# A forward transform that handles two slabs per step instead of one

## The chip, the cores and the metric

The kernel runs on one core of a Trainium2 chip. The metric is the device time of one launch in microseconds (us), taken as the median of several runs. A core has a matrix engine (TensorE, "PE" in the profile; its weight loads are the row "PEld"), a vector engine (VectorE, "DVE"), a scalar engine (ScalarE, "ACT"), a general engine (GpSimd, "POOL") and a synchronisation engine (SyncE, "SP"). Each has its own instruction queue and works it off in order. SP, ACT and POOL also issue DMA transfers. Matrix products read on-chip memory and write their sums into PSUM banks, which another engine then copies out.

## The reference, cut to what matters

The model has two layers over x of shape 4 x 512 x 128 x 64 (batch, time T, features, channels). The change touches only the second:

```python
trend = _moving_average(x, KERNEL)          # 25 wide, along time
seasonal = x - trend
xf = jnp.fft.rfft(seasonal, axis=1)
xs = xf[:, :M]                              # M = 128 modes
W = w_real + 1j * w_imag
ys = jnp.einsum('bmnc,cmk->bknc', xs, W)
...
filt = jnp.fft.irfft(yf, n=T, axis=1)
return trend + filt
```

The forward transform of the seasonal part is linear in x, so it can be a product of fixed matrices with x: for each batch, 128 modes, real and imaginary, from 512 times.

## The kernel before, in words

The first layer (`layer0`) runs until about 2795 us of the profile and is not touched. It ends by writing its result to `x4`, one DRAM tensor of 512 x 8192 per batch. The second layer (`layer1`, L845 on) treats two batches at a time (a group). For each group it runs three stages in a row: `transform` of both batches, `mix` (the channel-wise products with W), and `invert` of both batches. So there are two forward stages in the program, one from 2796 us to 2941 us and one from about 3292 us to 3437 us.

A batch is cut into 16 slabs of 512 columns. `transform` handles one slab per turn of its loop, 32 slabs per group:

- `slab` (L893) loads 512 x 512 values (1 MB) into an `xin` tile through SP. The tag "big" has five buffers, which `mix` also uses for its tiles `w` and `invert` for its own slabs.
- L906 and L907 (POOL queue) load the first and last 12 times of the slab, 24 rows, into an `edge` tile, and L908 (ACT) copies these rows to partitions 32 to 55, so that the same rows stand on two row groups of the array. `edge` has two buffers.
- L912 (DVE) forms the sum and the difference of the slab's two halves in time, `uv[0]` and `uv[1]`; L917 (DVE) forms sum and difference of the two halves of `uv[0]`, called `ev`. All of these have two buffers per tag.
- L921 (PE): four products of `uv[1]` with 64-column weights, the odd modes. L928 (PE): four products of `ev` with 32-column weights, the even modes. L935 (PE): four products of `edge` with 64-column weights on the row groups at 0 and 32, which correct the ends of the moving average. All twelve add into two PSUM banks `pf`, one real, one imaginary.
- L937 (ACT) copies the two banks into `xf`, the spectrum of the group, in which `mix` then reads every slab.

PSUM has four banks with the tag "a" and four with the tag "b". The forward transform uses only "a", that is, two slabs' worth. The order of PE's instructions is the order in which they are written (`manual_schedule`); for the other engines a scheduler places the instructions, and it may move one slab's work past another's where the buffers allow.

`mix` loads its weights `w` (1 MB each, L945, SP) into buffers of the tag "big", and POOL negates two parts of each at L948 before PE uses them. As built, POOL's queue has the first four of these negations between the edge loads of the last slabs: the order is edges of slab 27, `w` 0, edges of slab 28, `w` 1, edges of slab 29, `w` 2, edges of slab 30, `w` 3, edges of slab 31. PE's first products of `mix` are L955 and L959.

Of the kernel before, what the change touches and what calls it, by code (L numbers as in the profile page):

```python
# [10 lines left out]
F32 = mybir.dt.float32  # L11
AF = mybir.ActivationFunctionType
ALU = mybir.AluOpType
# [3 lines left out]
P = 128  # L17
T = 512
NF = 128
H = 64  # L20
D = NF * H
NCH = D // P
SL = 512
NS = D // SL
# [4 lines left out]
M = 128  # L29
KMA = 25  # L30
HALO = KMA // 2
# [813 lines left out]
def layer1(ctx, tc, x4, wri, dftv, dftd, dfte, idfte, idfto, avg, avgh, out):  # L845
# [7 lines left out]
    nc = tc.nc  # L853
# [5 lines left out]
    io = ctx.enter_context(tc.tile_pool(name="io", bufs=2))  # L859
# [4 lines left out]
    def load(pool, eng, name, src):  # L864
        t = pool.tile(list(src.shape), F32, name=name)
        eng.dma_start(t, src)
        return t

    dftv_sb = load(dft, nc.sync, "dftv_sb", dftv)
    dftd_sb = load(dft, nc.sync, "dftd_sb", dftd)  # L870
    dfte_sb = load(dft, nc.sync, "dfte_sb", dfte)
# [5 lines left out]
    def bank(tag):  # L877
        return ps.tile([P, SL], F32, tag=tag, name=tag)


    def by_c(row):
        return row.rearrange("p (a c l) -> p a l c", c=H, l=2)

    def by_n(row):
        return row.rearrange("p (a l c) -> p a l c", c=H, l=2)
# [7 lines left out]
    def slab(b, s):  # L893
        xin = io.tile([P, NT, SL], F32, tag="big", name="xin", bufs=5)
        nc.sync.dma_start(
            xin, x4[b][:, s * SL : (s + 1) * SL].rearrange("(c p) d -> p c d", p=P)
        )
        return xin

    def transform(b, xf):  # L900

        for s in range(NS):
            c = slice(s * SL, (s + 1) * SL)
            xin = slab(b, s)
            edge = io.tile([P, SL], F32, tag="edge", name="edge")
            nc.gpsimd.dma_start(edge[0:HALO, :], x4[b][0:HALO, c])  # L906
            nc.gpsimd.dma_start(edge[HALO : 2 * HALO, :], x4[b][T - HALO : T, c])  # L907
            nc.scalar.copy(edge[32 : 32 + 2 * HALO, :], edge[0 : 2 * HALO, :])  # L908
            uv = []
            for op in (ALU.add, ALU.subtract):  # L910
                t = io.tile([P, 2, SL], F32, tag=f"uv{len(uv)}", name="uv")
                nc.vector.tensor_tensor(t, xin[:, 0:2, :], xin[:, 2:4, :], op)  # L912
                uv.append(t)
            pf = [bank("a"), bank("a")]
            ev = io.tile([P, 2, SL], F32, tag="ev", name="ev")
            for k, op in enumerate((ALU.add, ALU.subtract)):
                nc.vector.tensor_tensor(ev[:, k, :], uv[0][:, 0, :], uv[0][:, 1, :], op)  # L917
            for i in range(2):
                for r in range(2):
                    h = 1 - r  # L920
                    nc.tensor.matmul(  # L921
                        pf[r][h * H : (h + 1) * H, :], lhsT=dftd_sb[:, i, r, :], rhs=uv[1][:, i, :],
                        start=(i == 0), stop=False,
                    )
            for k in range(2):
                for r in range(2):
                    q = r * H + k * H // 2
                    nc.tensor.matmul(  # L928
                        pf[r][q : q + H // 2, :], lhsT=dftv_sb[:, k, r, :], rhs=ev[:, k, :], start=True, stop=False
                    )  # L930
            for r in range(2):
                at = slice(32 * r, 32 * r + 2 * HALO)
                for h in range(2):
                    hs = slice(h * H, (h + 1) * H)
                    nc.tensor.matmul(pf[r][hs, :], lhsT=dfte_sb[at, hs], rhs=edge[at, :], start=False, stop=True)  # L935
            for r in range(2):
                nc.scalar.copy(by_c(xf[:, r, c]), by_n(pf[r]))  # L937

    def mix(xf):

# [83 lines left out]
    with tc.manual_schedule(engines={nc.tensor.engine}):  # L1024
        for b0 in range(0, B, G):
            xf = spec.tile([P, G, 2, D], F32, tag="xf", name="xf")
            for b in range(G):
                transform(b0 + b, xf[:, b, :, :])
            mix(xf)
            for b in range(G):  # L1030
                invert(b0 + b, xf[:, b, :, :])


def _constants():

    a = np.zeros((T, T))
    for t in range(T):
        for s in range(t - HALO, t + KMA - HALO):
            a[t, min(max(s, 0), T - 1)] += 1.0 / KMA
    around = np.zeros((T, T))  # L1040
    for t in range(T):
        for s in range(t - HALO, t + KMA - HALO):
            around[t, s % T] += 1.0 / KMA
    k, n = MODES, np.arange(T)
    angle = 2.0 * np.pi * ((k[:, None] * n[None, :]) % T) / T
    waves = np.stack([np.cos(angle), -np.sin(angle)])

    dft = waves @ (np.eye(T) - around)
    at = np.concatenate([np.arange(HALO), np.arange(T - HALO, T)])
    edge = (waves @ (around - a))[:, :, at]  # L1050
    dfte = np.zeros((2, 32, M))
    dfte[0, : 2 * HALO] = edge[0].T
    dfte[1, : 2 * HALO] = np.roll(edge[1], H, axis=0).T
    weight = np.where(k == 0, 1.0, 2.0)[:, None] / T
    idft = waves * weight
    idft[1, k == 0] = 0.0
    q = H // 2
    idfte = np.concatenate([idft[r, i : i + q, :P] for i in (0, q) for r in range(2)])
    idfto = np.concatenate([idft[r, H:, : T // 2] for r in range(2)])
    tiles = [slice(i * P, (i + 1) * P) for i in range(NT)]  # L1060
    avg = np.stack([a[s, s].T for s in tiles], axis=1)
    avgh = np.zeros((NT, 32, P))
    for j, s in enumerate(tiles):
        at = [t for t in range(s.start - HALO, s.start) if t >= 0]
        at += [t for t in range(s.stop, s.stop + HALO) if t < T]
        avgh[j, : len(at)] = a[s][:, at].T
    c = {
        "dftv": dft[:, :H, :P].reshape(2, 2, H // 2, P).transpose(3, 1, 0, 2),
        "dftd": dft[:, H:, : T // 2].reshape(2, H, 2, P).transpose(3, 2, 0, 1),
        "dfte": dfte.reshape(2 * 32, M),  # L1070
        "idfte": idfte,
        "idfto": idfto.reshape(M, 2, P),
        "avg": avg,
        "avgh": avgh.reshape(P, P),
    }
    return {n: v.astype(np.float32) for n, v in c.items()}


def _inputs(x, i):
# [22 lines left out]
    for rows, parts in ((MODES, ("w_real", "w_imag")), (IMAG, ("w_imag", "w_real"))):  # L1102
# [16 lines left out]
        "fb2": np.concatenate([i["ffn_b2"]] * 2)[:, None],  # L1119
        "wri": wri.reshape(H, M, 2, 2, M).transpose(1, 0, 2, 3, 4),  # L1120
        **_constants(),
    }
    return {n: np.ascontiguousarray(v) for n, v in a.items()}
# [17 lines left out]
```

## Time and profile before

| | |
|---|---|
| median of 3 runs | 3773.87 us (3772.81 to 3791.47) |
| span of the profiled execution | 3800.7 us |
| first forward stage, first product to first product of `mix` | 2804.05 to 2941.03 us |
| second forward stage, the same | 3297.58 to 3437.38 us |
| busy in 2880 to 2900 us | PE 20.00, DVE 18.87, ACT 8.91, POOL 5.01 us of 20 |
| moved by DMA in 2880 to 2900 us | 284 GB/s |
| median landing of an edge load | 4.6 us (L906), 4.4 us (L907) |

The profile is of one execution; its span is 0.7% longer than the median of the timed runs, and no separate time is given for that execution. All times in the text are counted from the start of that span. PE is busy 96% of the span, but busy time of a pipelined engine does not say that it is at its limit, so the stages have to be read one by one.

### The profile page before, as it was taken

What the parts mean: (1) busy time and instruction counts of PE and PEld (TensorE: products, weight loads), DVE (VectorE), ACT (ScalarE), POOL (GpSimd) and SP (SyncE); (2) the same over time, 40 slices, a digit from 0 to 9 for tenths busy, and PEclk for the clock granted to TensorE, in tenths of its full rate; (3) what the DMA queues carried; (4) which work ended last, traced back from release to release, by engine and by line L of the source; (5) the groups of instructions that cost most, each with busy time, mean ns of one, the idle gap of its engine ahead of it and who ended that gap; (6) DMA issues with size and microseconds to landing.
All of it is one profiled execution on the core that took longest, in us unless ns stands there. A gap on an engine that the chain in (4) does not pass through costs nothing. (4 is left out here: it accounts for less than half of the span.)

```text
span 3800.7 us, 44873 instructions
## 1 busy us (share of the span) xinstructions
PE 3636.3 (96%) x15945; PEld 1345.5 (35%) x15945; DVE 2683.6 (71%) x3498; ACT 1761.2 (46%) x2491; POOL 513.3 (14%) x782
## 2 busy tenths in 40 slices
PE   9989999999999999999999988999989999999998
PEld 4433322223333223333322322333322843327533
DVE  4445559976777896677789799755567277892677
ACT  0013336645656565566656678867744210142100
POOL 0000012210011221011122221100012000131001
PEclk9999989999999899999999999999999999999999
DMA  9867647786874788787478677545567478993687
GB/s 310 272 203 242 229 146 264 254 288 241 287 280 169 247 285 287 251 278 278 172 258 282 205 249 262 202 155 177 183 222 246 146 236 295 309 294 140 205 296 264
DMA packets 429175, 912.80 MB, mean 240 GB/s; under 512 B 33240, under 2 KB 83608, under 8 KB 424856
## 3 DMA queue, kind: packets, MB, share of 16 engines
q1 hardware_dynamic: 351024, 636.87, 49.7%
q0 software_dynamic: 75776, 271.62, 20.5%
q8 instruction: 127, 2.08, 0.2%
q10 hardware_dynamic: 2152, 1.45, 0.1%
q14 instruction: 96, 0.79, 0.1%
HBM read 641.31 MB, written 268.50 MB: 239 GB/s over the span
## 5 line engine op out<-in xcount | busy, mean ns | idle before, releaser
L729 PE MATMUL pa<-mid,w_sb 128*64 128x512 f32 x2048 | 500.2, 609 | 37.2 <-DVE x4t L734 37.2
L734 DVE SCALAR_TENSOR_TENSOR x4t<-pa,fb_sb,x 128x512 f32<-128x512 f32 x252 | 188.4, 748 | 345.7 <-PE pa L729 345.6
L722 ACT ACTIVATE mid<-m,fb_sb 128x1024 f32<-128x1024 f32 x256 | 285.1, 1114 | 280.5 <-PE m L718 280.2
L718 PE MATMUL m<-x,w_sb 64*128 64x512 f32 x1008 | 290.4, 649 | 0.4 <-ACT mid L722 0.4
L722 ACT ACTIVATE mid<-c,fb_sb 128x1024 f32<-128x1024 f32 x256 | 283.2, 1106 | 1.5 <-PE c L718 1.5
L718 PE MATMUL c<-x,w_sb 64*128 64x512 f32 x1008 | 263.4, 596 | 1.3 <-ACT mid L722 1.3
L729 PEld LDWEIGHTS pa<-mid,w_sb 128*64 128x64 f32 x2048 | 125.0, 136 | 379.9 <-issue 250.8
L406 PE MATMUL a<-xp,wx 128*128 128x512 f32 x512 | 240.7, 596 | 0.5 <-DVE me L268 0.5
L986 ACT COPY two<-a 128x512 f32<-128x512 f32 x64 | 37.5, 586 | 425.0 <-PE a L981 425.0
L1009 PE MATMUL b<-xin,avg_sb 128*128 128x512 f32 x512 | 230.8, 593 | 2.3 <-DVE xin L1015 2.3
L1015 DVE TENSOR_TENSOR xin<-b,pm 128x512 f32<-128x512 f32 x256 | 159.1, 684 | 95.6 <-PE b L1012 80.7
L567 ACT ACTIVATE sq<-x 128x1024 f32<-128x1024 f32 x128 | 135.0, 1054 | 180.5 <-DVE x L564 180.5
L620 DVE SCALAR_TENSOR_TENSOR to<-kd,vec,to 128x510 f32<-128x510 f32 (+1 forms) x272 | 197.8, 746 | 16.0 <-ACT to L616 10.4
L695 ACT ACTIVATE kd<-kd,vec 128x512 f32<-128x512 f32 x256 | 193.3, 809 | 3.1 <-DVE kd L687 3.1
L891 DVE COPY xf<-b 128x256 f32<-128x256 f32 x128 | 54.4, 425 | 185.3 <-PE b L955 173.2
L912 DVE TENSOR_TENSOR uv<-xin 128x1024 f32<-128x1024 f32 x128 | 155.4, 1227 | 39.4 <-DMA xin<-x 18.9
L251 PE MATMUL st<-x,ones 128*32 128x512 f32 x512 | 169.4, 611 | 13.3 <-DVE x L564 13.1
L743 PEld LDWEIGHTS pt<-ident,x4t 128*128 128x128 f32 x1024 | 107.7, 141 | 208.7 <-ACT mid L722 152.5
L528 DVE TENSOR_TENSOR x<-a,xp 128x1024 f32<-128x1024 f32 x128 | 156.2, 1220 | 33.6 <-PE a L526 31.1
L620 DVE SCALAR_TENSOR_TENSOR z<-x,vec,z 128x511 f32<-128x511 f32 x240 | 175.8, 745 | 5.7 <-ACT z L616 2.3
L526 PE MATMUL a<-rst,wo_sb 64*128 64x512 f32 x512 | 153.1, 672 | 27.2 <-DVE x L528 23.2
L743 PE MATMUL pt<-ident,x4t 128*128 128x128 f32 x1024 | 168.8, 288 | 1.5 <-ACT ob L750 1.5
(241 smaller groups left out, 6532.8 us busy)
## 6 DMA issues: line engine op xcount, KB each, us to landing
xp<-in_xt SPq DMA_DIRECT2D x256, 512.0 KB
xin<-x SPq DMA_DIRECT2D x128, 1024.0 KB
kh<-to SPq DMA_DIRECT2D x156, 512.0 KB
x<-x POOLq DMA_DIRECT2D x128, 512.0 KB, 4.4
kx<-x SPq DMA_DIRECT2D x128, 512.0 KB
x<-ob POOLq DMA_DIRECT2D x64, 1024.0 KB, 6.3
out<-xin POOLq DMA_DIRECT2D x64, 1024.0 KB, 7.1
x<-x SPq DMA_DIRECT2D x96, 512.0 KB
```

Of the source, the lines that this page charges most:

```text
L251: nc.tensor.matmul(st[32 * q : 32 * q + 32, :], lhsT=ones, rhs=src[:, j, :], start=first, stop=last,)
L406: nc.tensor.matmul(pa[:, k, :], lhsT=wq[:, j, k * P : (k + 1) * P], rhs=xp[:, j, :], start=first and j == 0, stop=last and j == 1,)
L528: nc.vector.tensor_tensor(x1, at, xp, ALU.add)
L620: tap = nc.vector.scalar_tensor_tensor(to[:, j, k:], xr[:, j, : SL - k], vec[:, w, c], to[:, j, k:], ALU.mult, ALU.add)
L695: tc.keep_in_program_order(nc.scalar.activation(d[:, j, :], d[:, j, :], AF.Identity, bias=vec[:, B4, c], scale=vec[:, G4, c]))
L718: nc.tensor.matmul(pm[:, h, :], lhsT=w1_sb[hs, m * P : (m + 1) * P], rhs=x3[hs, :], start=True, stop=True)
L722: nc.scalar.activation(mid, pm, AF.Gelu_apprx_tanh, bias=fb1_sb[:, m : m + 1])
L729: nc.tensor.matmul(pa[h * H : (h + 1) * H, :], lhsT=w2_sb[:, m, :], rhs=mid[:, h, :], start=(m == 0), stop=(m == 1),)
L734: nc.vector.scalar_tensor_tensor(x4t, pa, fb2_sb, x3s[c // 2][:, c % 2, :], ALU.add, ALU.add)
L743: nc.tensor.transpose(pt[:, t, :], x4t[:, t * P : (t + 1) * P], ident)
L1009: nc.tensor.matmul(po[j], lhsT=avg_sb[:, j, :], rhs=xin[:, j, :], start=True, stop=False)
L1015: nc.vector.tensor_tensor(by_n(xin[:, j, :]), by_n(po[j]), by_c(pm[j % 2][:, j // 2, :]), ALU.add)
```

## The change

The loop now takes two slabs per turn (a pair). One `edge` tile holds the edge rows of both slabs, at partitions 0 and 32 for the first and at 64 and 96 for the second, and the weights `dfte` are stored twice so that they stand on all four row groups. The edge loads and their ACT copies are as many as before. On VectorE the same four operations per slab are made, with the difference (now `v`) written ahead of the sum (now `u`) in the program. On TensorE the products of a pair come by kind: eight of L921's kind, eight of L928's, then eight edge products, which use four row groups and two column halves. Pairs use the PSUM tags "a" and "b" in turn, four banks each. The copies out of PSUM come after the pair.

```diff
--- before.py
+++ after.py
@@ -899,42 +899,55 @@
 
     def transform(b, xf):
 
-        for s in range(NS):
-            c = slice(s * SL, (s + 1) * SL)
-            xin = slab(b, s)
+        for g in range(NS // 2):
             edge = io.tile([P, SL], F32, tag="edge", name="edge")
-            nc.gpsimd.dma_start(edge[0:HALO, :], x4[b][0:HALO, c])
-            nc.gpsimd.dma_start(edge[HALO : 2 * HALO, :], x4[b][T - HALO : T, c])
-            nc.scalar.copy(edge[32 : 32 + 2 * HALO, :], edge[0 : 2 * HALO, :])
-            uv = []
-            for op in (ALU.add, ALU.subtract):
-                t = io.tile([P, 2, SL], F32, tag=f"uv{len(uv)}", name="uv")
-                nc.vector.tensor_tensor(t, xin[:, 0:2, :], xin[:, 2:4, :], op)
-                uv.append(t)
-            pf = [bank("a"), bank("a")]
-            ev = io.tile([P, 2, SL], F32, tag="ev", name="ev")
-            for k, op in enumerate((ALU.add, ALU.subtract)):
-                nc.vector.tensor_tensor(ev[:, k, :], uv[0][:, 0, :], uv[0][:, 1, :], op)
-            for i in range(2):
-                for r in range(2):
-                    h = 1 - r
-                    nc.tensor.matmul(
-                        pf[r][h * H : (h + 1) * H, :], lhsT=dftd_sb[:, i, r, :], rhs=uv[1][:, i, :],
-                        start=(i == 0), stop=False,
-                    )
+            uv, ev, pf = [], [], []
+            for k in range(2):
+                s = 2 * g + k
+                c = slice(s * SL, (s + 1) * SL)
+                xin = slab(b, s)
+                q = k * H
+                nc.gpsimd.dma_start(edge[q : q + HALO, :], x4[b][0:HALO, c])
+                nc.gpsimd.dma_start(edge[q + HALO : q + 2 * HALO, :], x4[b][T - HALO : T, c])
+                nc.scalar.copy(edge[q + 32 : q + 32 + 2 * HALO, :], edge[q : q + 2 * HALO, :])
+                u = io.tile([P, 2, SL], F32, tag="uv0", name="u")
+                v = io.tile([P, 2, SL], F32, tag="uv1", name="v")
+                nc.vector.tensor_tensor(v, xin[:, 0:2, :], xin[:, 2:4, :], ALU.subtract)
+                nc.vector.tensor_tensor(u, xin[:, 0:2, :], xin[:, 2:4, :], ALU.add)
+                t = io.tile([P, 2, SL], F32, tag="ev", name="ev")
+                for i, op in enumerate((ALU.add, ALU.subtract)):
+                    nc.vector.tensor_tensor(t[:, i, :], u[:, 0, :], u[:, 1, :], op)
+                uv.append(v)
+                ev.append(t)
+                pf.append([bank("ab"[g % 2]), bank("ab"[g % 2])])
+            for k in range(2):
+                for i in range(2):
+                    for r in range(2):
+                        h = 1 - r
+                        nc.tensor.matmul(
+                            pf[k][r][h * H : (h + 1) * H, :], lhsT=dftd_sb[:, i, r, :], rhs=uv[k][:, i, :],
+                            start=(i == 0), stop=False,
+                        )
+            for k in range(2):
+                for i in range(2):
+                    for r in range(2):
+                        q = r * H + i * H // 2
+                        nc.tensor.matmul(
+                            pf[k][r][q : q + H // 2, :], lhsT=dftv_sb[:, i, r, :], rhs=ev[k][:, i, :],
+                            start=True, stop=False,
+                        )
             for k in range(2):
                 for r in range(2):
-                    q = r * H + k * H // 2
-                    nc.tensor.matmul(
-                        pf[r][q : q + H // 2, :], lhsT=dftv_sb[:, k, r, :], rhs=ev[:, k, :], start=True, stop=False
-                    )
-            for r in range(2):
-                at = slice(32 * r, 32 * r + 2 * HALO)
-                for h in range(2):
-                    hs = slice(h * H, (h + 1) * H)
-                    nc.tensor.matmul(pf[r][hs, :], lhsT=dfte_sb[at, hs], rhs=edge[at, :], start=False, stop=True)
-            for r in range(2):
-                nc.scalar.copy(by_c(xf[:, r, c]), by_n(pf[r]))
+                    at = slice(k * H + 32 * r, k * H + 32 * r + 2 * HALO)
+                    for h in range(2):
+                        hs = slice(h * H, (h + 1) * H)
+                        nc.tensor.matmul(
+                            pf[k][r][hs, :], lhsT=dfte_sb[at, hs], rhs=edge[at, :], start=False, stop=True
+                        )
+            for k in range(2):
+                s = 2 * g + k
+                for r in range(2):
+                    nc.scalar.copy(by_c(xf[:, r, s * SL : (s + 1) * SL]), by_n(pf[k][r]))
 
     def mix(xf):
 
@@ -1067,7 +1080,7 @@
     c = {
         "dftv": dft[:, :H, :P].reshape(2, 2, H // 2, P).transpose(3, 1, 0, 2),
         "dftd": dft[:, H:, : T // 2].reshape(2, H, 2, P).transpose(3, 2, 0, 1),
-        "dfte": dfte.reshape(2 * 32, M),
+        "dfte": np.concatenate([dfte.reshape(2 * 32, M)] * 2),
         "idfte": idfte,
         "idfto": idfto.reshape(M, 2, P),
         "avg": avg,
```

## The prediction

> **What bounds the kernel now.** I read the page first: PE is busy 96% of the span, which settles nothing. The chain that ended last, cut to the first forward stage, shows what that stage waits for:
>
> ```profile
> 2876.36 1.87 PE a L921 x8
> 2878.23 1.00 PE a L928 x8
> 2879.22 1.02 PE a L935 x8
> 2880.24 1.87 PE a L921 x8
> ...
> 2913.20 1.24 DVE uv L912
> 2914.44 0.02 issue
> 2914.45 4.12 DMA w<-in_wri
> 2918.57 0.50 POOL edge L906
> 2919.07 4.50 DMA edge<-x
> 2923.57 0.14 issue
> 2923.70 2.44 PE a L935 x8
> 2926.15 3.61 PE a L921 x8
> ```
>
> The columns are start, length in us, and what was late. PE alone carries the chain: 1.87 + 1.00 + 1.02 = 3.88 us a slab. Near the end a detour appears: an edge load stands behind a negation of `w` in POOL's queue, that behind the load of `w`, so PE gets its edge rows late, and then runs at half speed. From the first product of slab 1 (2811.21) to that of slab 28 (2918.98) a slab takes 107.8 / 27 = 3.99 us.
>
> Second, how near the next engines are. The windows view (busy us of PE, PEld, DVE, ACT, POOL; granted clock, DMA share, GB/s) and VectorE's timeline while PE does not yet hold it back:
>
> ```profile
> 2880.00:2900.00 20.00, 20.00 (x126) 4.44 (x124) 18.87 (x22) 8.91 (x15) 5.01 (x10) 1.00 0.91 284
> ```
>
> ```profile
> 2828.46 2.36 DVE L912 TENSOR_TENSOR uv<-xin 128x1024 f32<-128x1024 f32 x2
> 2830.74 1.29 DVE L917 TENSOR_TENSOR ev<-uv 128x512 f32<-128x512 f32 x2
> 2832.06 2.36 DVE L912 TENSOR_TENSOR uv<-xin 128x1024 f32<-128x1024 f32 x2
> 2834.34 1.29 DVE L917 TENSOR_TENSOR ev<-uv 128x512 f32<-128x512 f32 x2
> 2835.66 2.36 DVE L912 TENSOR_TENSOR uv<-xin 128x1024 f32<-128x1024 f32 x2
> ```
>
> The reader is to see the step from one first L912 to the next: 3.60 us. VectorE needs 3.60 us a slab, TensorE 3.88. Whatever TensorE gains beyond 0.28 us a slab, VectorE keeps.
>
> Third, TensorE's timeline, for how products on several row groups go, and what an idle TensorE pays:
>
> ```profile
> 3107.02 1.14 PE L1012 MATMUL b<-halo,avgh_sb 12*128 12x512 f32 x8
> 3108.09 1.13 PE L981 MATMUL a<-xf,idfte_sb 64*128 64x512 f32 x4
> ```
>
> ```profile
> 3323.04 2.42 PE L935 MATMUL a<-edge,dfte_sb 24*64 24x512 f32 x8 [1.81 <-DMA edge<-x]
> 3325.39 3.68 PE L921 MATMUL a<-uv,dftd_sb 128*64 128x512 f32 x8
> 3329.00 1.90 PE L928 MATMUL a<-ev,dftv_sb 128*32 128x512 f32 x8
> ```
>
> L1012 is four products on four row groups, and the next kind starts 1.07 us later: all four run at once. After 1.81 us of idling the second group runs at half speed: 3.68 for 1.94, 1.90 for 1.06.
>
> **What the Trainium skill says.** "TensorEngine Tiling (Array Packing)", section Key Properties: changing the tiling mode, not just the tile, drains the engine. The trace agrees. A full-width 256-column product in `mix` starts every 0.43 us, so 512 columns take 0.86; L921's two rounds of two column halves would be 1.72 and take 1.87, one round of L928 takes 1.00 and of L935 1.02: about 0.15 us at each change of kind. The same page's Available Configurations gives 32x64 tiles as eight independent ones; the trace shows four of them together (L935) and four row groups together (L1012), never eight. "VectorE: DVE Perf Modes", section Mode 2×_2P, says that an fp32 `tensor_tensor` stays at one element per cycle; all of VectorE's forward work is of this kind, and no row shows it faster. "TensorE: Matmul & The Clock Gate", Part 1, says that the clock is halved after an idle window of about 3.4 us, watched freely running; here 1.53 to 1.81 us of idling before a broken-up L935 sufficed.
>
> **The change part by part.** Sums are differences against the profiled execution (span 3800.7 us, 26.8 us over the median); I subtract them from the median.
>
> *TensorE, a pair.* L921's kind: four rounds of 0.86 plus 0.15 = 3.59. L928's kind: two rounds plus 0.15 = 1.86. Edges: one round, 1.02, if eight tiles run at once. Together 6.47 us against 2 x 3.88 = 7.76. If the eight do not overlap beyond four, the edges take 1.87 and the pair 7.3.
>
> *VectorE, a pair.* The operations are the same. As built, the order settles into u, u, v, v, then the four `ev`. Back to back the starts lie 1.14 us apart after an L912 and 0.61 after a first L917, 0.71 at the return: 4 x 1.14 + 3 x 0.61 + 0.71 = 7.1, against 7.2 by the measured 3.60. I take 7.15. Each waits for products one pair back: with D the start of a VectorE pair, L921's kind runs from D+3.45 to D+6.9, L928's to D+8.7, edges to D+9.7; `v` of the next pair is wanted at D+9.4, `ev` at D+11.7. So VectorE never waits, TensorE idles about 0.7 us a pair, and the pair takes 7.15.
>
> *DMA.* 2 MB and the edge rows per 7.15 us are 307 GB/s. From 3295 to 3335 us the core moved 339 GB/s on average while VectorE waited for slabs. A slab's buffer is now held 2.3 us longer (from u to its v), but a reload has 12 us or more. I cost it at nothing; if loads only reach 290 GB/s, the pair takes 7.6.
>
> *Edge loads, ACT, PSUM.* As many as before, now two pairs of buffers: from the end of one edge round to need there are some 13 us for 2 us of issuing, 4.6 of landing, 1.24 of copying. Before it was under 7, and edges were late at 2817 to 2857 us and 3303 to 3323 us. That lateness goes into VectorE's pace. ACT does 2 x 0.62 + 4 x 0.58 = 3.6 us a pair; banks alternate between "a" and "b", so the copies have over 5 us to spare.
>
> *Start of a stage.* First slabs arrive when DMA delivers (DVE starts at 2801.48 and 2808.14): unchanged. From 2808.14, slabs 1 to 7 at 3.6 us plus about 1 us for v waiting on slab 5 end at 2834.3; eleven more pairs put the last pair's start at D = 2834.3 + 11 x 7.15 = 2913.0. In the second stage slab 7 is there at 3325.2 (before: same wait); then v, v and the `ev` end at 3331.2, D = 3409.9.
>
> *End of a stage.* As built, POOL has the first two `w`s negated ahead of the last pair's four edge loads, and ACT has that pair's edge copies ahead of the previous pair's four copies to `xf`. `w` 1 gets its buffer at D-3.7, lands 4 to 5 us later, its negations (2.1 to 2.9 us for two, as at 2915 and 2920) end at D+3.5, four loads are issued by D+5.6, landed by D+10.0, copied by D+10.7. Edges wait about 1.7 us (D+8.7 was possible) and end at D+11.6; then ACT's four and three more copies bring `mix` to D+14.8. First stage 2927.8 instead of 2941.03, second 3424.7 instead of 3437.38: -13.2 and -12.7. TensorE idles about 3 us before `mix`, so its first products run at half clock: +2 each, by the 1.6 to 2.6 us that such spells cost (L921 and L928 above). Sum: -25.9 + 4 = -22 us.
>
> **Rivals.** *A: the pair stays slower than VectorE's 7.15.* Either the eight tiles share (7.3) or DMA gives 290 GB/s (7.6). For it: no row shows eight tiles, and DMA share is 0.91 already; against: L1012, and 339 GB/s. At 7.6, 0.45 x 22 = 10 us are lost: 3762.
>
> *B, slower: the clock.* TensorE's new 0.7 us gap in every pair could let the clock gate close, which a TensorE without gaps never risked. A spell costs 1.74 + 0.83 = 2.6 us (rows above), so a pair with one takes 6.47 + 2.6 = 9.1, 1.9 above VectorE's. With 28 pairs the gain of 22 is gone when four pairs in ten have one; at two thirds, +36 - 22 = 3788; at all, 3804. For it: half clock came after 1.5 us. Against: 0.57 us at 3312.8 did nothing, and five sixths of any pair are work.
>
> *C: more.* If `mix` starts warm and its first tail is shorter (edge loads landing in 2 us, the least seen), 4 + 5 come on top, with 7.1 a pair another 1: 3742.
>
> **How the numbers follow.** Forecast 0.62: 3773.9 - 22 = 3752, its own range 3744 to 3761. A 0.14 (3757 to 3767), B 0.12, C 0.12. A measurement of this kernel tells a change from none at about 0.5%, 18.9 us, that is below 3755. The forecast lies close to that border: two thirds of it below gives 0.42, with C 0.12 and a little of A 0.02: faster 0.56. Same 0.20 + 0.12 = 0.32, slower 0.12. Range 3741 to 3772: it takes in A and C and leaves out B.
>
> **What would show it.** L921's first product to the next pair's: 7.1 to 7.2 us in mid-stage; VectorE's share there near 1 with no waits on PE; PE idle 0.7 a pair waiting for `v`; edge rounds of eight products 1.0 us apart from the next kind; clock 1.00. First product of `mix` near 2928 and 3425, after 3 us of ACT copies. Edge rounds of 1.9, waits of VectorE on `xin` or clock below 1 in mid-stage would prove A or B; a last edge round without delay, C.

## The result, and the profile after

| | before | after |
|---|---|---|
| median of 7 runs | 3773.68 us (3772.04 to 3791.47) | 3764.65 us (3747.07 to 3773.79) |
| ratio, 95% interval | | 0.9966 [0.9947, 0.9985] |
| span of the profiled execution | 3800.7 us | 3763.9 us |

The changed kernel is 9.0 us or 0.34% faster. That is a gain, as its interval leaves out 1, but a smaller one than the 0.5% that the prediction took as the least that a measurement tells from none. The forecast of 3752 us is 12.7 us too low. The two profiled executions differ by four times as much as the medians. So the first thing to read is in which layer they differ. The program has fixed marks: the last transpose product of the first layer (L743), the first product of each forward stage, the first product of `mix`, the first product of `invert`. From the end of the first mark and the starts of the others in the timeline of TensorE (us):

| stretch | before | after | difference |
|---|---|---|---|
| first layer, not touched | 2795.32 | 2779.23 | -16.1 |
| first forward stage, to the first product of `mix` | 145.72 | 133.98 | -11.7 |
| first `mix` | 111.44 | 114.01 | +2.6 |
| `invert` and second forward stage | 384.91 | 371.30 | -13.6 |
| second `mix` | 111.44 | 113.71 | +2.3 |
| second `invert` | 251.90 | 251.71 | -0.2 |
| second layer | 1005.4 | 984.7 | -20.7 |

In the second layer, where the change was made, 20.7 us are gone; the other 16.1 us of the profiled difference are in code that is the same in both programs.

In the middle of the forward stage the windows view of the changed kernel (busy us of PE, PEld, DVE, ACT, POOL; clock, DMA share, GB/s) answers to the line of the kernel before:

```profile
2840.00:2860.00 20.00, 18.81 (x143) 5.48 (x136) 20.00 (x24) 10.29 (x18) 6.01 (x12) 1.00 0.99 319
```

VectorE is busy for 20.00 of 20 us where it was 18.87, and TensorE for 18.81 where it was 20.00: they have changed places. The timeline of TensorE in the changed kernel (start, length, line, tile, count of recorded passes, and in brackets the idle time and what ended it) shows the pair:

```profile
2842.31 3.65 PE L927 MATMUL b<-v,dftd_sb 128*64 128x512 f32 x16 [0.40 <-DVE v L915]
2845.90 1.92 PE L935 MATMUL b<-ev,dftv_sb 128*32 128x512 f32 x16
2847.75 1.11 PE L944 MATMUL b<-edge,dfte_sb 24*64 24x512 f32 x16
2849.27 3.65 PE L927 MATMUL a<-v,dftd_sb 128*64 128x512 f32 x16 [0.40 <-DVE v L915]
```

From one first L927 to the next are 6.96 us. TensorE works through its three kinds and then idles 0.40 us for a `v`. All eight edge products, which are recorded as sixteen passes, take one round of 1.11 us. The timeline of VectorE in the same kernel shows the same pace and no gap:

```profile
2887.33 2.35 DVE L916 TENSOR_TENSOR u<-xin 128x1024 f32<-128x1024 f32 x2
2889.60 2.35 DVE L915 TENSOR_TENSOR v<-xin 128x1024 f32<-128x1024 f32 x2
2891.87 2.49 DVE L919 TENSOR_TENSOR ev<-u 128x512 f32<-128x512 f32 x4
2894.28 2.35 DVE L916 TENSOR_TENSOR u<-xin 128x1024 f32<-128x1024 f32 x2
```

A pair is 2894.28 - 2887.33 = 6.95 us. The line at 2894.28 opens the last pair of the stage, the D of the prediction. VectorE's last operation ends at 2901.31.

The end of the stage is in the chain of waits of the changed kernel (start, length, what was late):

```profile
2897.80 4.16 DMA w<-in_wri
2901.95 0.74 POOL w L961 x2
2902.70 0.50 POOL edge L910
2903.19 4.96 DMA edge<-x
...
2908.89 0.61 ACT edge L912
2909.50 0.03 issue
2909.53 3.64 ACT xf L950 x7
```

The detour of the kernel before is still here: `mix` (2913.21) waits for copies, these for the last pair's edge rows, these for a place in POOL's queue behind negations of `w`. The first line needs care. It is inferred from the time of an event, and the load that it names was issued at 2897.80 as the fourth `w`, while only the first two are negated ahead of the edge loads. Their loads were issued at 2885.03 and 2890.85, and taking the landing events in order of issue they were in place at 2893.48 and 2895.95. What POOL did meanwhile is in its timeline, of which these are two single instructions, the first negation and the fourth:

```profile
2893.71 7.87 POOL L961 TENSOR_SCALAR w<-w 128x256 f32<-128x256 f32 x1 [7.43 <-DVE ev L919]
2902.29 0.41 POOL L961 TENSOR_SCALAR w<-w 128x256 f32<-128x256 f32 x1
```

The same operation takes 0.41 us once VectorE is done and 7.87 us while VectorE works without a gap; it ends at 2901.58, 0.27 us after VectorE's last operation. The second stage repeats it: 8.74 us, ending 0.27 us after VectorE. Two such negations took 2.90 and 2.12 us in the kernel before, whose VectorE waited a little for TensorE (0.19 us) in every slab; there each of them waited for one operation of VectorE, not for a row.

### The profile page after: what moved, and what is told of

It is laid out like the page before. It is cut to its first block, busy times and chain, and to the rows that moved or that the text cites. A ratio compares the mean times of both kernels' runs of the same rounds, so it can differ in the third digit from the quotient of the medians.

```text
span 3763.9 us, 44885 instructions
## 1 busy us (share of the span) xinstructions
PE 3579.2 (95%) x15945; PEld 1343.9 (36%) x15945; DVE 2673.8 (71%) x3498; ACT 1758.2 (47%) x2491; POOL 520.8 (14%) x782
## 3 DMA queue, kind: packets, MB, share of 16 engines
q0 software_dynamic: 75776, 271.62, 20.7%
## 5 line engine op out<-in xcount | busy, mean ns | idle before, releaser
L743 PEld LDWEIGHTS pt<-ident,x4t 128*128 128x128 f32 x1024 | 107.6, 141 | 208.7 <-ACT mid L722 152.5
L743 PE MATMUL pt<-ident,x4t 128*128 128x128 f32 x1024 | 168.8, 288 | 1.5 <-ACT ob L750 1.5
L565 POOL DMA_DIRECT2D x<-x x128 | 93.6, 731 | 547.4 <-DVE x L564 501.0
```

The source lines that it names most:

```text
L743: nc.tensor.transpose(pt[:, t, :], x4t[:, t * P : (t + 1) * P], ident)
```

## The experiments: two questions

First: why did the median move by 9 us when the layer that was changed moved by 21? Either the length of the first layer varies from execution to execution in both programs, or the changed program shifts it. Second: what set the end of each forward stage, and would the stage be shorter without it? The theory is that POOL's stalled negations hold the last edge loads; the rival is that the last pair ends late for the sake of VectorE, TensorE or the copies anyway.

**Both kernels again.** No edit.

> The kernel before, once more, to be read beside the changed one on the same chip. Theory 1 (the gain is made in the two forward stages and the rest of the spread comes from the granted clock in the first layer): its second layer lasts as in the profile of before, 1005 us from the last product of the first layer to the end, and only the first layer differs, by the windows at half clock. Theory 2 (the change costs the first layer something): the first layer of the kernel before is shorter than the changed kernel's by some 10 us at the same number of half-clock windows. Expected ratio 1.00.

> The changed kernel once more. Theory 1: second layer 984 to 986 us (the two traces differ there by 20.6 us), forward pairs every 6.95 us; time 8 to 21 us under before, with the runs spread over some 25 us and the granted clock falling as the time rises. Theory 2: first layer longer than in the kernel before by some 10 us whatever the clock.

In five rounds on one chip the kernel before gave 3784.21 us as a run of its own (ratio to itself 1.0004 [0.9993, 1.0015]) and the changed one 3764.22, ratio 0.9951 [0.9936, 0.9966], that is -19 us. By the marks in their traces, beside two other runs that are introduced below:

| run | first layer, us | of it at half clock, us | second layer, us |
|---|---|---|---|
| before | 2795.32 | 153.6 | 1005.4 |
| before again | 2776.01 | 99.0 | 1004.3 |
| before, pinned | 2767.78 | 99.0 | 995.1 |
| after | 2779.23 | 112.6 | 984.7 |
| after again | 2790.21 | 150.2 | 982.9 |
| after, pinned | 2774.53 | 105.8 | 963.7 |

The first layer of either program takes anything from 2768 to 2795 us; it is longest where the clock record has most time at half clock, in the kernel before as in the changed one. The clock explains most of it and not all: half of the 54.6 us between the most and the least time at half clock is 27.3 us, and the layers differ by 27.5, but two layers with the same 99.0 us differ by 8.2. No shift by the change is to be seen, and the first comparison of profiles (-36.8 us) had a long first layer on one side. The second layer repeats within 2 us: -20.7 the first time, -21.4 the second. In timed runs only the whole time and the mean granted clock are known. The second comparison agrees with the second layer's loss; the first, whose interval allows at most 20.0 us, gives less. The changed kernel took the same in both (3764.65 and 3764.22 us). It is the kernel before that differed: 3773.68 us in the first, 3783.66 in the second. In the second its median granted clock was 0.980; in the experiments on another chip further below it was 0.983, and the time 3773.65. By an estimate from these figures, 0.003 of 3780 us is 11 us, about as much as the two comparisons differ by. For the kernel before in the first comparison the clock isn't on record, so that this was the reason there is likely and not shown.

**Negations behind the edge loads.** In the changed kernel and in the kernel before the first five `w` are negated in program order, which puts them behind the last edge loads in POOL's queue. Nothing else is different: the same instructions, the same work on the other engines.

```diff
-                nc.gpsimd.tensor_scalar(t, t, -1.0, 0.0, ALU.mult, ALU.add)
+                flip = nc.gpsimd.tensor_scalar(t, t, -1.0, 0.0, ALU.mult, ALU.add)
+                if g < 5:
+                    tc.keep_in_program_order(flip)
```

> The changed kernel with the negations of the first five w pinned behind all edge loads in POOL's queue; nothing else moves. Theory 1 (the last pair's edge loads stand behind a negation that VectorE's two-input operations lock out until they end): the last edge round starts about 8.4 us after the start of the last VectorE pair instead of 14, mix starts 11 to 12 us after it instead of 18.9 and 25.2, which is -7 and -13 us, and its first products run at full clock, another -2 each: about -20 us against the changed kernel. Rival (mix is then late for its negated w, or ACT's copies hold it anyway): less than 8 us.

> The kernel before with the same pin. Theory: the late edge load of slab 28 and the half clock after it go; mix starts 4 to 6 us sooner in each stage, about -10 us in all. Rival: the edge loads of the last slabs are late for another reason (their landing), and nothing above 3 us comes of it.

The changed kernel with this edit took 3744.62 us (3740.00 to 3746.24), ratio to before 0.9893 [0.9880, 0.9906]; no other kernel of this study is as fast. Its POOL timeline, with the first eight negations taken together:

```profile
2887.91 0.50 POOL L911 DMA_DIRECT2D edge<-x  x1
2889.23 10.13 POOL L961 TENSOR_SCALAR w<-w 128x256 f32<-128x256 f32 x8 [0.81 <-DVE ev L919]
```

and its TensorE timeline at the end of the stage:

```profile
2893.10 3.65 PE L927 MATMUL b<-v,dftd_sb 128*64 128x512 f32 x16 [0.40 <-ACT edge L912]
2896.69 1.92 PE L935 MATMUL b<-ev,dftv_sb 128*32 128x512 f32 x16
2898.54 1.11 PE L944 MATMUL b<-edge,dfte_sb 24*64 24x512 f32 x16
2901.33 0.70 PE L970 MATMUL b<-xf,w 128*128 128x256 f32 x2 [1.68 <-ACT xf L950]
```

The first negation is held as before, 7.54 of the 10.13 us for eight, but nothing that is wanted soon stands behind it: the last edge load has been issued at 2887.91. The last edge products follow without a gap and `mix` starts 11.9 us after D = 2889.47, where it took 18.9. In the second stage it is 11.9 against 19.4. (The 25.2 us in the expectation for the second stage were not counted from the start of the last pair, 3379.09; from there it is 19.4.) That is 7.0 and 7.5 us, with a first `mix` at full clock another 2.6 (111.45 us for 114.01). Against the repeat of the changed kernel, whose `mix` came 17.6 and 19.1 us after D, it is 5.7 and 7.2, and 1.6 for `mix`. The second layer as a whole is 19 to 21 us shorter than in these two runs. About 3 us of the rest lie between the start of `invert` and the last pair of the second stage (348.9 us, against 351.9 and 352.2), and their cause stays open. In the kernel before the same pin gives 9 to 10 us, ratio 0.9975 [0.9961, 0.9988]. The theory holds: the place in the queue costs both kernels, and the changed one twice as much. The rival falls: with the edge rows in time, neither VectorE, TensorE nor the copies keep `mix` beyond those 11.9 us.

**Which engine sets the pair.** The next three were run together, on another chip. One leaves the edge products in two rounds of four, so that TensorE has 7.6 us of work a pair and VectorE the same operations as in the changed kernel, though the scheduler places them in another order. The other two take work from VectorE.

```diff
                             start=True, stop=False,
                         )
-            for k in range(2):
                 for r in range(2):
                     at = slice(k * H + 32 * r, k * H + 32 * r + 2 * HALO)
```

Here the edge products of a slab stand in the loop over `k` of its even products: even, edge, even, edge.

> The changed kernel with the even and the edge products written one slab at a time (even 0, edge 0, even 1, edge 1): the edge products of the two slabs no longer meet on four row groups, and there are two more changes of kind. Theory 1 (a pair takes the longer of TensorE's chain and VectorE's 6.95 us): TensorE's chain becomes 3.58 + 2 x 1.00 + 2 x 1.02 = 7.6 us, so TensorE is the bound again, a pair takes 7.6 to 7.7 us, and each forward stage is some 9 us longer. Rival (VectorE alone sets the pace and grouping is worth nothing beyond the two halves of L927): pairs stay at 6.95.

It took 3760.36 us, ratio 0.9970 [0.9954, 0.9986], with a second layer of 983.6 us: no slower than the changed kernel in full (984.7 and 982.9). TensorE's timeline in it:

```profile
2841.20 3.65 PE L927 MATMUL b<-v,dftd_sb 128*64 128x512 f32 x16
2844.78 1.06 PE L935 MATMUL b<-ev,dftv_sb 128*32 128x512 f32 x8
2845.78 1.09 PE L943 MATMUL b<-edge,dfte_sb 24*64 24x512 f32 x8
2846.80 1.06 PE L935 MATMUL b<-ev,dftv_sb 128*32 128x512 f32 x8
2847.79 1.09 PE L943 MATMUL b<-edge,dfte_sb 24*64 24x512 f32 x8
2848.81 1.51 PE L927 MATMUL a<-v,dftd_sb 128*64 128x512 f32 x6
```

The pair takes 7.61 us as expected, and no line shows idle time: TensorE carries the stage again. But the 9 us a stage that were to follow from it did not. VectorE now waits for products, up to 0.33 us at a time, and its negations are not held for the row:

```profile
2891.64 1.22 POOL L960 TENSOR_SCALAR w<-w 128x256 f32<-128x256 f32 x2 [2.13 <-issue]
2891.64 0.42 POOL L960 TENSOR_SCALAR w<-w 128x256 f32<-128x256 f32 x1 [2.13 <-issue]
```

```profile
2890.57 1.23 DVE L915 TENSOR_TENSOR v<-xin 128x1024 f32<-128x1024 f32 x1 [0.33 <-PE b L927]
2891.71 1.69 DVE L919 TENSOR_TENSOR ev<-u 128x512 f32<-128x512 f32 x2
```

Two negations take 1.22 us (the second line is the first of them alone), and 1.53 in the second stage. They don't fall into VectorE's gaps: the first ends at 2892.06, 0.26 us after the `v`, while the `ev` behind that `v` follows without a gap. So each waits for one operation of VectorE, where in the changed kernel one waits for ten. The edge loads behind them are issued in time, the last edge products follow their `ev` without a gap, TensorE idles 0.69 us before each `mix`, and both `mix` run at full clock (111.44 us). First stage 137.5 us against 134.0 and 132.4, both `mix` together 222.9 against 227.7 and 226.3, the second stage equal: what the slower pair loses, the quick end gives back. POOL's order is the same, two `w` ahead of the last edges; what is new is VectorE's row, its gaps and its order (`v`, `ev`, `ev`, `u`, `ev`, `ev`, `u`, `v`, for `u`, `u`, `v`, `v` and four `ev`). Which of the two lets the negations in isn't told apart.

The other edit leaves out the difference of each slab's `ev` pair, and its products read the sum instead, so that the result is not the transform any more. It is shown for the changed kernel; in the kernel before it is the same.

```diff
-                for i, op in enumerate((ALU.add, ALU.subtract)):
-                    nc.vector.tensor_tensor(t[:, i, :], u[:, 0, :], u[:, 1, :], op)
+                nc.vector.tensor_tensor(t[:, 0, :], u[:, 0, :], u[:, 1, :], ALU.add)
...
-                            pf[k][r][q : q + H // 2, :], lhsT=dftv_sb[:, i, r, :], rhs=ev[k][:, i, :],
+                            pf[k][r][q : q + H // 2, :], lhsT=dftv_sb[:, i, r, :], rhs=ev[k][:, 0, :],
```

> The changed kernel without the second of the two ev operations of each slab (the difference is left out, its products read the sum): VectorE has 5.75 us of work a pair instead of 6.95, TensorE has the same. Theory 1 (VectorE is the bound of the changed kernel): the pair falls to TensorE's chain, 6.5 to 6.6 us; and as VectorE then has gaps, a negation on POOL behind which edge loads stand takes under 2 us each instead of 7.9 and 8.7, so that mix starts about 13 us after the last VectorE pair begins. Rival A (loads are the bound): pairs stay near 6.95. Rival B (the long negations wait for something other than VectorE): they stay near 8 us.

> The kernel before without the second ev operation of each slab, left out in the same way: VectorE 2.9 us a slab instead of 3.60. Theory 1 (TensorE alone bounds the kernel before in mid-stage): slabs stay at 3.88 us and each stage at its length within 2 us but for its end, where the negations find gaps sooner. Rival (VectorE's load already held slabs back): slabs faster by 0.1 us or more.

With one `ev` operation fewer for each slab the changed kernel took 3751.15 us (ratio 0.9943 [0.9928, 0.9958]), its second layer 965.4 us; the kernel before took 3773.35 us (0.9992 [0.9980, 1.0003]), its second layer 993.7. TensorE's timeline of the changed kernel with less:

```profile
2840.18 3.65 PE L926 MATMUL a<-v,dftd_sb 128*64 128x512 f32 x16
2843.77 1.92 PE L934 MATMUL a<-ev,dftv_sb 128*32 128x512 f32 x16
2845.62 1.11 PE L943 MATMUL a<-edge,dfte_sb 24*64 24x512 f32 x16
2846.66 1.51 PE L926 MATMUL b<-v,dftd_sb 128*64 128x512 f32 x6
```

and of the kernel before with less:

```profile
2835.50 1.94 PE L920 MATMUL a<-uv,dftd_sb 128*64 128x512 f32 x8
2837.36 1.07 PE L927 MATMUL a<-ev,dftv_sb 128*32 128x512 f32 x8
2838.36 1.09 PE L934 MATMUL a<-edge,dfte_sb 24*64 24x512 f32 x8
2839.38 1.94 PE L920 MATMUL a<-uv,dftd_sb 128*64 128x512 f32 x8
```

In the changed kernel the pair falls from 6.95 to 6.48 us and the 0.40 us of idling are gone: that is TensorE's own chain. The loads are then close: the core moves 353 GB/s, and VectorE waits 0.3 to 0.4 us a pair for `xin` on average. In the kernel before the slab stays at 3.88 us. Its second layer gains 11 us (993.7 against 1004.3), and that is at the end of the stages: two negations take 1.2 to 1.4 us, and the two slabs that took 6.69 and 5.66 us (second stage 7.40 and 6.17) in the repeat of the kernel before take 3.88 each. So in the middle of a stage TensorE alone bounded the kernel before, and VectorE alone bounds the changed one. One expectation missed: in the changed kernel with less, `mix` did not start 13 us after the last pair began but about as late as before. The negations took only 1.94 us for two, as expected, but began at 2896.42, and the edge loads behind them were issued from 2899.61 and took about 6 us to land. They began late because their `w` was late: issued at 2885.21, it was in place at 2896.18, 11.0 us later, where the changed kernel's took 8.5. So the place in the queue costs time even when the negations themselves run fast.

## Why the prediction came out as it did

| step of the prediction | predicted | measured |
|---|---|---|
| TensorE's chain of a pair | 6.47 us | 6.48 (with less work on VectorE) |
| eight edge products | one round, 1.02 | one round, 1.04 (2845.62 to 2846.66) |
| pair, set by VectorE | 7.15 | 6.95 |
| TensorE idle a pair | 0.7 | 0.40 |
| clock in the middle of the stage | 1.00 | 1.00 |
| DMA in the middle | 307 GB/s, costs nothing | 319 GB/s, no wait of VectorE on `xin` |
| first stage: D after the end of layer 1 | 117.7 | 115.05 |
| second stage: D after the start of `invert` | 357.4 | 351.9 |
| `mix` after D | 14.8 and 14.8 | 18.9 and 19.4 |
| half clock at the start of `mix` | +2 each | +2.6 and +2.3 |
| second layer | -22 | -20.7 and -21.4 |

**What held.** The change of bound, the eight tiles at once, the open clock gate and the free transfers. Rival A falls by the edge round of 1.04 us and the 319 GB/s, rival B by the clock of 1.00 with a gap of 0.40 us in every pair. Rival C's premise, a warm and short end, did not occur in the changed kernel; the pinned version brought it about on purpose, and was 39 us under the kernel before of the same comparison (3783.66), where C had 32.

**What was off, first term: the pair.** I took 7.15 us, between 7.1 from the starts of single operations and 7.2 from the measured slab. By the lines shown above the starts lie 1.14 us apart for the four operations on `xin` and 0.60 for the four `ev`, the return from the last `ev` to the next `u` included, for which the prediction had 0.71 from a VectorE with gaps. Eleven pairs at 0.2 less are 2.2 us in each stage. In the second stage D was 5.5 early, and 5.2 in the repeat; the rest is in the start of the stage, which the prediction had left as it was. In the first trace VectorE waited less for its first slabs (2.7 us on `xin` between the first product and steady pace, 6.9 in the kernel before), but in the repeats it was 5.4 and 5.8, so that isn't shown to be the reason.

**What was off, second term: the end.** The step that failed is "its negations (2.1 to 2.9 us for two, as at 2915 and 2920) end at D+3.5". The `w` was loaded when the prediction said: issued at D-3.4, in place at D+1.7. But the first negation was held to D+7.3, all four ended at D+8.4, the edge loads were issued by D+10.4 and landed near D+14, and `mix` came at D+18.9. The duration came from a kernel in which VectorE had gaps, and the same prediction said that VectorE would have none. The row was right for its own kernel and its condition was taken away by the change. The Trainium skill describes such a stall, in "SBUF — State Buffer", section "🔬 SBUF: two separate sides": VectorE and GpSimd share one pair of ports to on-chip memory as an exclusive lock, and an operation that needs it (a VectorE operation with two inputs there does, against a GpSimd operation that reads there) keeps it for its whole length while the other engine stands still. The kernels with gaps in VectorE's work agree: each of their negations waited for one operation of VectorE at most. The changed kernel goes further: one waiting instruction was passed over for a whole row of ten and eleven, 7.87 and 8.74 us, and so again in its repeat and with the pin. Why a row without gaps shuts GpSimd out, while between two operations of another row it gets in without a gap, no run here shows.

**The sum.** The two terms nearly cancel: D early by 2.7 and 5.5, `mix` late by 4.1 and 4.6 after it. So -20.7 beside -22 is closer than its terms deserve, and that is luck. The median's -9 beside that is no step of the sum: the prediction took the difference in the second layer for the difference in the time, and gave its range no part for the first layer, which moves by up to 27 us between executions of programs in which it is the same. Two small slips in its sums carry no weight: with the edge rows copied by D+10.7 the wait beyond D+8.7 is 2.0 us and not 1.7, and rival B with a spell in every pair comes to 3805 and not 3804.

## What to carry to other kernels

A duration of a GpSimd operation is only good for the load that VectorE had when it was measured: here, once VectorE had no gaps left, a negation of 0.40 us waited for the end of VectorE's row, and all that stood behind it in GpSimd's queue, DMA issues too, waited with it. So keep transfers that are needed soon ahead of GpSimd arithmetic that is not, which here was worth as much as the whole change. And where a gain is some tenths of a per cent, compare it stretch by stretch between fixed marks of the program before believing the total, in either direction.

## What the runs showed of the hardware

An in-place negation on GpSimd of 128 x 256 values takes 0.40 us with VectorE at rest. Against a gapless row of two-input VectorE operations (20.00 of 20 us busy) the first to arrive took 7.5 to 8.8 us in six of six stages, and ended 0.27 us after the row. In the runs whose VectorE had gaps the first four of a stage took 0.4 to 1.5 us each. They cost VectorE time too: two `ev` with a negation let in before each took 1.69 us, for 1.28 without. GpSimd's DMA issues were not held: beside the same gapless row they took 0.50 us each, as elsewhere.

Eight products of 24 rows and 64 columns on four row groups and two column halves took as long together (1.04 us) as four do (1.02). A TensorE that idled for 1.68 us before `mix`, after an edge round at half speed (3.24 us for 1.11) that followed 4.86 us of idling, ran 114.0 us of `mix` for 111.4; after 1.68 us of idling behind warm products it ran the first `mix` in 111.45 us, and the second in 113.12 after 1.67 us: nearly the same gap was paid for once and not the other time. In a stretch of the program that no edit touched, the time at half clock went from 99 to 154 us, and the stretch from 2768 to 2795 us.
